# Even states of a selective scan take B from transposes of a repeated column; side work issued in fewer, later pieces

## The chip, the cores and the metric

The kernel runs on 1 core of one Trainium2 chip, in one launch. The metric is device time in microseconds from the first to the last instruction of that core; the time before is the median of 3 runs, 5304.8 us (5303.92 to 5304.85).

## The reference

Two layers, each added to its input after a group norm. Layer 0, in which the change lies, is a two-dimensional selective scan; layer 1 is a spectral attention block that is the same in both kernels. Layer 0, cut to what matters here:

```python
xin, z = split(x @ in_proj_w.T)                    # 4 images of 48 x 48 positions, d = 256
xc = silu(depthwise_conv3x3(xin) + conv_b)
xs = [xc, xc transposed, xc reversed, xc transposed and reversed]   # 4 directions, L = 2304
x_dbl = einsum('bkdl,kcd->bkcl', xs, x_proj_w)     # 40 rows: 8 for dt, 16 for B, 16 for C
dt = softplus(einsum('bkrl,kdr->bkdl', x_dbl[:8], dt_proj_w) + dt_proj_b)
for l in range(L):                                 # 16 states for each of the 256 channels
    h = h * exp(dt[l] * A) + (dt[l] * xs[l]) * B[l]
    y[l] = sum over the states of h * C[l]
y = the four directions, turned back and added, + Ds * xs
out = (layernorm(y) * silu(z)) @ out_proj_w.T
```

## The kernel before, in words

Channels lie on the 128 partitions in two halves (f = 0, 1), positions along the free axis. Each of 4 images has 4 directions in the order 0, 2, 1, 3 (ORDER), each direction 5 chunks of 480 positions (the last of them 384), each chunk 16 states: 80 chunks, 1280 states.

*The states.* The scan over positions is one DVE instruction per state over both halves (scan, L610), with a gap of two columns between them that carries the state from chunk to chunk. What goes into it:
- the decay, exp(dt * A), from ACT (decay, L598);
- the drive, dt * x * B. An **even** state makes it on DVE: spread (L549) copies one row of B to all partitions of the PSUM tile pb by a bf16 matmul of the chunk's tile bs with a column of pick, and drive_in (L568) multiplies du by pb into db. An **odd** state (turned) makes it on ACT and PE: scale (L575) multiplies dut, which is du transposed, by a column of bt, which is B transposed, and turn (L585) transposes the product into the PSUM tile da with 8 PE transposes.

After the scan, read_out (L619) multiplies h by C on POOL into hc (C is read back from memory, spread over the partitions, by fetch, L544), carry_on (L624) keeps the last column, and sum_up (L629) adds hc into the PSUM tiles yp with 8 PE transposes per state that accumulate. After state 15, put_away (L681) copies yp out on ACT, into the tile that held dut.

*The order.* The kernel writes out its own order: `on.` keeps every engine's instructions in the order of issue (so all of them have line L54 in the profile). advance (L735) takes one state per step and calls each stage for the state that entered so many steps before:

```python
    LAGS = (
        (3, fetch), (8, put_away), (4, drive_in), (5, scan), (4, decay_here), (3, spread), (4, turn), (3, decay_there),
        (2, extra), (2, scale), (5, read_out), (5, carry_on), (7, sum_up),
    )
```

*Side work.* What is not a state is written as generators that wait in the list later; piece (L708) runs one of them to its next yield. advance runs one piece at the end of every step, and extra (L719) one more in steps of odd states: three pieces for two states. A generator that yields FREE lets another one in; one that yields nothing goes on at the next piece. drain (L723) runs pieces until a generator is done. The generators:
- project_chunk (L400), for a chunk of the next direction: px (the 40 rows of x_dbl, and B twice more), the copies xd and bs, the products with less, dt from two pd matmuls, and bt from the transposes pt. bs holds B in bf16 with its first and second remainder, on rows 0, 64 and 96; the two products with less subtract from px what bs already holds, so that pick can add three bf16 parts to one nearly exact float32 row.
- turn_du (L375), which transposes du for the odd states, started by turning (L764);
- gather (L647), which turns yp's copy back and adds it to the direction before;
- back (L465), the layer norm and the output projection of a finished chunk, in direction 3;
- front (L265), input projection and convolution of the next image, and matrices (L288), which prepares layer 1 beside the last image; boot (L236) for the first.

All side matmuls go to one PSUM bank (tag pp, side, L152), which ACT or DVE must empty before the next one. The loop from L779 drives all this: in states 6 and 10 (or 9 and 12 of a direction's last chunk) it multiplies du for the next chunk on POOL (drive, L456), and after the second of these it calls turning, which first drains unfinished gathers.

Of the kernel before, what the change touches and what calls it, by code (L numbers as in the profile page):

```python
# [10 lines left out]
F32 = mybir.dt.float32  # L11
BF16 = mybir.dt.bfloat16
AF = mybir.ActivationFunctionType
ALU = mybir.AluOpType
# [8 lines left out]
D = 256  # L23
NF = D // 128
N = 16
R = 8
K = 4
NX = 112
BANK = 512
NH = 32  # L30

# [26 lines left out]
def first_layer(ctx, tc, io, x1_dram, sp_dram, d_w, d_m):  # L58
# [11 lines left out]
    small = ctx.enter_context(tc.tile_pool(name="l0_small", bufs=2))  # L70
    one = ctx.enter_context(tc.tile_pool(name="l0_one", bufs=1))
    two = ctx.enter_context(tc.tile_pool(name="l0_two", bufs=2))
    three = ctx.enter_context(tc.tile_pool(name="l0_three", bufs=3))
    four = ctx.enter_context(tc.tile_pool(name="l0_four", bufs=4))
    ring = ctx.enter_context(tc.tile_pool(name="l0_ring", bufs=RING))
    ps_a = ctx.enter_context(tc.tile_pool(name="l0_psa", bufs=1, space=PSUM))
# [26 lines left out]
    nc.scalar.dma_start(cb, io["conv_b"].rearrange("(f p) -> p f", p=128))  # L103

    w_xp = const.tile([128, K, NF, NX], F32, name="w_xp")
    on.gpsimd.memset(w_xp, 0.0)
    w_x = one.tile([128, K, NF, R + 2 * N], F32, tag="y", name="w_x")
    for k in range(K):
        nc.sync.dma_start(w_x[:, k], io["x_proj_wT"][k].rearrange("(f p) c -> p f c", p=128))
    for o, c0, c1 in ((0, R, R + 2 * N), (32, 0, R), (64, R, R + N), (96, R, R + N)):  # L110
        on.vector.tensor_copy(w_xp[:, :, :, o : o + c1 - c0], w_x[:, :, :, c0:c1])

    pick = const.tile([NX, N], BF16, name="pick")
    p3 = one.tile([NX, N], F32, tag="y", name="p3")
    on.vector.tensor_add(p3, ident[0:NX, 0:N], ident[0:NX, 64 : 64 + N])
    on.vector.tensor_add(pick, p3, ident[0:NX, 96 : 96 + N])

    less = const.tile([NX, 2, NX], BF16, name="less")
    on.gpsimd.memset(less, 0.0)
    on.vector.tensor_scalar(less[:, 0, 64:NX], ident[0:NX, 64:NX], -1.0, None, ALU.mult)  # L120
    on.vector.tensor_scalar(less[:, 1, 96:NX], ident[0:NX, 96:NX], -1.0, None, ALU.mult)
    b_dt = const.tile([128, K, NF], F32, name="b_dt")
    nc.scalar.dma_start(b_dt, io["dt_proj_b"].rearrange("k (f p) -> p k f", p=128))
    a_neg = const.tile([128, K * NF, N], F32, name="a_neg")
# [27 lines left out]
    def side(name):  # L152
        pool, tag = banks[0]
        if not begun[0]:
            banks.rotate(-1)
        return pool.tile([128, 512], F32, tag=tag, name=name)
# [218 lines left out]
    def turn_du(c):  # L375
# [3 lines left out]
        for h in range(0, 4, 2):  # L379
# [11 lines left out]
            for q, m, r in some:  # L391
                o = (q - h) * 256
                on.scalar.copy(c.dut[0:r, q : q + m], p[0:r, o : o + m * 256].rearrange("p (q d) -> p q d", d=256))

    def load_dt(b, k):
        w_dt = one.tile([32 + R, D], F32, tag="w_dt", name=f"w_dt{b}_{k}")
        nc.sync.dma_start(w_dt[32 : 32 + R], io["dt_proj_wT"][k])
        return w_dt

    def project_chunk(c, w_dt, xc):  # L400


        k, s, n = c.k, c.s, c.n
        src = at(xc, k, s, n)
        px = side(f"px{c.t}")
        for f in range(NF):
            on.tensor.matmul(
                like(px[0:NX, 0:n], k), w_xp[:, k, f], src[:, f], start=(f == 0), stop=(f == NF - 1)
            )
            yield  # L410
        xd = one.tile([32 + R, LC], F32, tag="xd", name=f"xd{c.t}")
        on.scalar.copy(xd[:, 0:n], px[0 : 32 + R, 0:n])
        c.cd = dram.tile([2 * N, LC], F32, tag="cd", name=f"cd{c.t}")
        nc.sync.dma_start(c.cd[:, 0:n], xd[0 : 2 * N, 0:n])

        c.bs = ring.tile([NX, LC], BF16, tag="bs", name=f"bs{c.t}")
        on.scalar.copy(c.bs[:, 0:n], px[0:NX, 0:n])
        for q in range(2):
            on.tensor.matmul(px[0:NX, 0:n], less[:, q], c.bs[:, 0:n], start=False, stop=True, skip_group_check=True)
            yield  # L420
            rows = slice(64 + 32 * q, NX)
            on.scalar.copy(c.bs[rows, 0:n], px[rows, 0:n])
        c.dt = ring.tile([128, NF, LC], F32, tag="dt", name=f"dt{c.t}")
        for f in range(NF):
            pd = side(f"pd{c.t}_{f}")
            on.tensor.matmul(
                pd[:, 0:n],
                w_dt[32 : 32 + R, f * 128 : (f + 1) * 128],
                xd[32 : 32 + R, 0:n],
                start=True,  # L430
                stop=True,
            )
            yield
            on.scalar.activation(c.dt[:, f, 0:n], pd[:, 0:n], AF.Identity, bias=b_dt[:, k, f : f + 1])

        c.bt = ring.tile([LB, 4, N], F32, tag="bt", name=f"bt{c.t}")
        pt = side(f"pt{c.t}")
        for q, r in blocks(n):
            on.tensor.transpose(pt[0:r, q * N : (q + 1) * N], xd[0:N, q * LB : q * LB + r], ident[0:N, 0:N])
        yield  # L440
        for q, m, r in runs(n):
            on.scalar.copy(c.bt[0:r, q : q + m], pt[0:r, q * N : (q + m) * N].rearrange("p (q n) -> p q n", n=N))

    def project(b, k, chunks, xc):

# [103 lines left out]
    def spread(u):  # L549

        c, i, n = u.c, u.i, u.c.n
        if i == N - 1:
            done[0] = c.number + 1
        if u.turned:
            return
        u.pb = ps_b.tile([128, 512], F32, tag="pb", name=f"pb{c.t}_{i}")
        on.tensor.matmul(
            u.pb[:, 0:n], pick[:, i : i + 1].to_broadcast([NX, 128]), c.bs[:, 0:n], start=True, stop=True
        )
        u.db = two.tile([128, NF * (LC + GAP)], F32, tag="db", name=f"db{c.t}_{i}")  # L560
        on.gpsimd.tensor_copy(u.db[:, n : n + GAP], before(u))

    def before(u):

# [53 lines left out]

    def read_out(u):  # L619
        c, i, n = u.c, u.i, u.c.n  # L620
        u.hc = three.tile([128, NF, LC], F32, tag="hc", name=f"hc{c.t}_{i}")
        on.gpsimd.tensor_mul(u.hc[:, :, 0:n], halves(u.h, n), u.cbc[:, :, 0:n].to_broadcast([128, NF, n]))

    def carry_on(u):  # L624
# [4 lines left out]
    def sum_up(u):  # L629

        c, i, n = u.c, u.i, u.c.n
        if i == 0:
            c.yp = [ps_y.tile([128, 512], F32, tag=f"yp{q}", name=f"yp{c.t}_{q}") for q in range(2)]
        for q, r in blocks(n):
            for f in range(NF):
                o = q % 2 * 256 + f * 128
                on.tensor.matmul(
                    c.yp[q // 2][0:r, o : o + 128],
                    u.hc[:, f, q * LB : q * LB + r],
                    ident,  # L640
                    start=(i == 0 and q % 2 == 0 and f == 0),
                    stop=(i == N - 1),
                    is_transpose=True,
                    skip_group_check=True,
                )

    def gather(c, yt):  # L647

# [68 lines left out]
                return  # L717

    def extra(u):  # L719
        if u.turned:  # L720
            piece()

    def drain(gen):  # L723
# [3 lines left out]

    decay_here, decay_there = partial(decay, turned=False), partial(decay, turned=True)
    LAGS = (
        (3, fetch), (8, put_away), (4, drive_in), (5, scan), (4, decay_here), (3, spread), (4, turn), (3, decay_there),  # L730
        (2, extra), (2, scale), (5, read_out), (5, carry_on), (7, sum_up),
    )
    window = deque([None] * 9, 9)

# [44 lines left out]
    for j, chunks in enumerate(directions):  # L779
        b, k = chunks[0].b, chunks[0].k  # L780
        if k == ORDER[0]:
            coming = None
        if k == ORDER[-1]:
            if b + 1 < B:
                drain(coming)
            images[b]["x"] = load_x(b, "xr")
        nxt = upcoming(j + 1) if j + 1 < len(directions) else None
        on.gpsimd.memset(carries[j % 2], 0.0)
        for m, c in enumerate(chunks):
            c.carry = carries[j % 2]  # L790
            for i in range(N):
                if k == ORDER[0] and b + 1 < B and m > 1 and coming is None and not any(g in later for g in backs):
                    coming = front(b + 1, images[b + 1])
                    later.append(coming)
                if k == ORDER[0] and b + 1 == B and m > 1 and coming is None and not any(g in later for g in backs):
                    coming = matrices()
                    later.append(coming)
                ahead = None
                if m + 1 < len(chunks):
                    f = (6, 10).index(i) if i in (6, 10) else None  # L800
                    if f is not None:
                        while not (j or chunks[m + 1].ready):
                            piece()
                        ahead = chunks[m + 1]
                elif nxt is not None:
                    f = (9, 12).index(i) if i in (9, 12) else None
                    if f is not None:
                        drain(nxt)
                        ahead = directions[j + 1][0]
                if ahead is not None:  # L810
                    drive(ahead, f)
                    if f:
                        turning(ahead)
                advance(Step(c, i))
                if not chunks[-1].ready and not j:
                    piece()
# [1288 lines left out]
```

## Time and profile before

| | |
|---|---|
| median of 3 runs | 5304.8 us |
| the profiled execution | 5305.0 us, span 5302.9 us |
| scans, first to last | from 80 to 4481 us |
| layer 1 after that | to 5303 us |
| mean granted TensorE clock | 0.870 |
| POOL waits for an hc that yp still reads | 261.3 us |
| PE waits for the copies of bs ahead of px<-bs,less | 151.1 us |
| DVE waits for pb ahead of db | 329.6 us |

The profile is of one execution. Engines: PE is the matmul side of TensorE and PEld its weight loads, which overlap; DVE is VectorE, ACT ScalarE, POOL GpSimd. A group of instructions is written out<-in by tile names. In brackets or after the bar stands the time that an engine was idle just before an instruction, with the instruction that ended it. The shares of the whole span are means over stretches with different limits, so a stretch is read by its own numbers. One float32 matmul call that is no transpose shows as two records; a transpose shows as one.

### The profile page before, as it was taken

Reading aid. Unit: us, or ns where it says so; the run is one execution under the profiler, and the core shown is the slowest. Engines: PE = TensorE matmul, PEld = TensorE weight load, DVE = VectorE, ACT = ScalarE, POOL = GpSimd, SP = SyncE. Lnnn points to the kernel's source line nnn. Section 1 sums busy time; section 2 is a strip of 40 time slices with the busy share of each in tenths; the row PEclk is TensorE's granted clock in tenths of the full one; section 3 lists DMA queues with packets and bytes.
Section 4 is the critical chain, followed back from the end, with each engine's and each line's share of the span. In section 5 each row is a group of like instructions: output and inputs, shape, how many; then the busy total and the mean of one; then the engine's idle time right before and its main releaser. Section 6 shows DMA issues by size and latency. Waiting matters only on the chain. (4 is left out here: it accounts for less than half of the span.)

```text
span 5302.9 us, 70751 instructions
## 1 busy us (share of the span) xinstructions
PE 4352.1 (82%) x24396; PEld 3035.5 (57%) x24396; DVE 3838.3 (72%) x2580; ACT 3771.0 (71%) x7327; POOL 3362.2 (63%) x3534
## 2 busy tenths in 40 slices
PE   6779888788798987888889888787888777688976
PEld 2556666555566666555666656565666655254543
DVE  1457778877787878768788777777888786456636
ACT  3667788878787878887888788877888876323344
POOL 2356767766777777766777677676777675146631
PEclk8879889888888888889899888988889898799977
DMA  1112222222222222222223222233333223216546
GB/s 33 53 51 68 83 70 81 76 70 67 76 76 84 76 75 74 75 66 85 70 78 87 74 72 74 67 88 74 84 85 86 71 78 88 54 28 160 127 117 152
DMA packets 306194, 417.78 MB, mean 79 GB/s; under 512 B 110804, under 2 KB 285012, under 8 KB 305260
## 3 DMA queue, kind: packets, MB, share of 16 engines
q1 hardware_dynamic: 300256, 410.19, 28.9%
q8 instruction: 193, 3.16, 0.2%
q10 hardware_dynamic: 5580, 3.08, 0.2%
q14 instruction: 165, 1.35, 0.1%
HBM read 377.99 MB, written 35.38 MB: 78 GB/s over the span
## 5 line engine op out<-in xcount | busy, mean ns | idle before, releaser
L54 POOL TENSOR_TENSOR hc<-h,cbc 128x960 f32<-128x960 f32 (+1 forms) x1280 | 2543.6, 1987 | 1280.0 <-DVE h L54 619.1
L54 DVE TENSOR_TENSOR_SCAN h<-da,carry,db 128x962 f32<-128x962 f32 (+1 forms) x640 | 1360.8, 2126 | 495.7 <-ACT da L54 465.4
L54 PEld LDWEIGHTS yp<-ident,hc 128*128 128x128 f32 (+1 forms) x9728 | 1259.9, 155 | 510.6 <-issue 366.2
L54 PE MATMUL yp<-ident,hc 128*128 128x128 f32 (+1 forms) x9728 | 1430.6, 299 | 22.2 <-POOL hc L54 17.0
L54 DVE TENSOR_TENSOR_SCAN h<-decay,carry,da 128x962 f32<-128x962 f32 (+1 forms) x640 | 1364.2, 2132 | 61.2 <-PE da L54 33.0
L54 ACT ACTIVATE scaled<-turned,bt 128x256 f32<-128x256 f32 (+1 forms) x2432 | 1036.1, 497 | 1.7
L54 DVE TENSOR_TENSOR db<-du,pb 128x960 f32<-128x960 f32 (+1 forms) x640 | 705.2, 1102 | 392.0 <-PE pb L54 329.6
L54 ACT ACTIVATE da<-dt,a_neg 128x480 f32<-128x480 f32 (+1 forms) x1280 | 827.2, 646 | 158.9 <-DVE h L54 137.3
L54 PE MATMUL da<-ident,scaled 128*128 128x128 f32 (+1 forms) x4864 | 711.8, 293 | 210.2 <-DVE h L54 174.2
L54 PEld LDWEIGHTS da<-ident,scaled 128*128 128x128 f32 (+1 forms) x4864 | 624.9, 156 | 434.8 <-ACT scaled L54 133.1
L54 ACT ACTIVATE decay<-dt,a_neg 128x480 f32<-128x480 f32 (+1 forms) x1280 | 790.9, 665 | 0.4
L54 PE MATMUL pc<-pad,cdiag 128*128 128x480 f32 (+1 forms) x630 | 290.6, 572 | 10.9 <-ACT pad L54 6.8
L54 POOL TENSOR_TENSOR du<-dt,xc 128x480 f32<-128x480 f32 (+1 forms) x160 | 206.3, 1290 | 108.1 <-ACT dt L54 108.1
L54 PE MATMUL pd<-xd,w_dt 8*128 8x480 f32 (+1 forms) x320 | 238.6, 837 | 35.5 <-ACT dt L54 18.2
L54 PE MATMUL pb<-bs,pick 112*128 112x480 bf16 (+1 forms) x640 | 251.4, 393 | 10.9 <-DVE db L54 10.7
L54 PE MATMUL px<-xc,w_xp 128*112 128x480 f32 (+1 forms) x320 | 223.8, 789 | 18.4 <-ACT xc L54 12.2
L1522 PE MATMUL acc<-v,attn_c 128*64 128x384 f32 x1152 | 210.3, 501 | 27.9 <-POOL v L1518 14.0
L54 ACT ACT_TABLE_LOAD x147 | 188.6, 1283 | 58.6 <-PE gv_l L54 34.9
L1518 POOL TENSOR_TENSOR v<-grep,xrep 128x768 f32<-128x768 f32 x96 | 174.7, 1823 | 87.4 <-PE acc L1522 46.9
L54 PEld LDWEIGHTS da<-carry,ident 128*128 128x128 f32 x1280 | 221.7, 217 | 0.0
L1514 DVE TENSOR_TENSOR v<-gp,xrep 128x1536 f32<-128x1536 f32 x96 | 168.1, 1756 | 73.9 <-PE acc L1522 41.2
L54 PE MATMUL da<-carry,ident 128*128 128x2 f32 x1280 | 211.5, 235 | 0.0
(382 smaller groups left out, 4544.8 us busy)
## 6 DMA issues: line engine op xcount, KB each, us to landing
cbc<-cd SPq DMA_DIRECT2D x1024, 240.0 KB
cbc<-cd SPq DMA_DIRECT2D x256, 192.0 KB
xrep<-dxt SPq DMA_DIRECT2D x48, 576.0 KB
grep<-dgt SPq DMA_DIRECT2D x16, 576.0 KB
x<-in_xT SPq DMA_DIRECT2D x16, 288.0 KB
xr<-in_xT SPq DMA_DIRECT2D x16, 288.0 KB
da_m<-a_m SPq DMA_DIRECT2D x24, 192.0 KB
a_m<-da_m SPq DMA_DIRECT2D x32, 144.0 KB
```

What stands on the lines that cost most here:

```text
L54: return lambda *args, **kw: self._tc.keep_in_program_order(emit(*args, **kw))
L1514: nc.vector.tensor_mul(v, gp[:, None, :, 0:NC].to_broadcast([128, 2, 2, NC]), x[:, :, 0:2])
L1518: nc.gpsimd.tensor_mul(v3, r[:, 2:3].to_broadcast([128, 2, NC]), x[:, :, 2])
L1522: nc.tensor.matmul(acc[c][64 * b : 64 * b + 64, 0:NC], attn_c[:, 2 * pair + b, g, q], v[:, b, c] if c < 2 else v3[:, b], start=first, stop ...
```

## The change

- **B for even states.** bs, less and pick go. spread makes pb with one PE transpose per block of 128 positions, whose input is one column of bt repeated 128 times. NX falls from 112 to 40.
- **bt.** The four transposes pt and their own yield go; in each of the two pd pieces two blocks of xd are transposed by an ordinary matmul with ident into spare columns of the same bank. w_dt becomes a constant tile with zeros in rows 0 to 31, and pd contracts over all 40 rows of xd instead of the 8 rows from 32. project_chunk has 4 yields instead of 7.
- **Side pieces on demand.** extra runs only where more than one generator waits.
- **turning** is called in state 13 instead of after the second drive.
- **The order in a step.** The sum of an even state has lag 8, so both sums of a pair stand in one step; put_away comes last; the copy of the carry into db is a stage of its own (open_db, lag 2) ahead of read_out instead of behind spread. hc has four buffers instead of three.

```diff
--- before.py
+++ after.py
@@ -25,7 +25,7 @@
 N = 16
 R = 8
 K = 4
-NX = 112
+NX = 40
 BANK = 512
 NH = 32
 
@@ -70,7 +70,6 @@
     small = ctx.enter_context(tc.tile_pool(name="l0_small", bufs=2))
     one = ctx.enter_context(tc.tile_pool(name="l0_one", bufs=1))
     two = ctx.enter_context(tc.tile_pool(name="l0_two", bufs=2))
-    three = ctx.enter_context(tc.tile_pool(name="l0_three", bufs=3))
     four = ctx.enter_context(tc.tile_pool(name="l0_four", bufs=4))
     ring = ctx.enter_context(tc.tile_pool(name="l0_ring", bufs=RING))
     ps_a = ctx.enter_context(tc.tile_pool(name="l0_psa", bufs=1, space=PSUM))
@@ -103,22 +102,12 @@
     nc.scalar.dma_start(cb, io["conv_b"].rearrange("(f p) -> p f", p=128))
 
     w_xp = const.tile([128, K, NF, NX], F32, name="w_xp")
-    on.gpsimd.memset(w_xp, 0.0)
     w_x = one.tile([128, K, NF, R + 2 * N], F32, tag="y", name="w_x")
     for k in range(K):
         nc.sync.dma_start(w_x[:, k], io["x_proj_wT"][k].rearrange("(f p) c -> p f c", p=128))
-    for o, c0, c1 in ((0, R, R + 2 * N), (32, 0, R), (64, R, R + N), (96, R, R + N)):
+    for o, c0, c1 in ((0, R, R + 2 * N), (32, 0, R)):
         on.vector.tensor_copy(w_xp[:, :, :, o : o + c1 - c0], w_x[:, :, :, c0:c1])
 
-    pick = const.tile([NX, N], BF16, name="pick")
-    p3 = one.tile([NX, N], F32, tag="y", name="p3")
-    on.vector.tensor_add(p3, ident[0:NX, 0:N], ident[0:NX, 64 : 64 + N])
-    on.vector.tensor_add(pick, p3, ident[0:NX, 96 : 96 + N])
-
-    less = const.tile([NX, 2, NX], BF16, name="less")
-    on.gpsimd.memset(less, 0.0)
-    on.vector.tensor_scalar(less[:, 0, 64:NX], ident[0:NX, 64:NX], -1.0, None, ALU.mult)
-    on.vector.tensor_scalar(less[:, 1, 96:NX], ident[0:NX, 96:NX], -1.0, None, ALU.mult)
     b_dt = const.tile([128, K, NF], F32, name="b_dt")
     nc.scalar.dma_start(b_dt, io["dt_proj_b"].rearrange("k (f p) -> p k f", p=128))
     a_neg = const.tile([128, K * NF, N], F32, name="a_neg")
@@ -392,8 +381,10 @@
                 o = (q - h) * 256
                 on.scalar.copy(c.dut[0:r, q : q + m], p[0:r, o : o + m * 256].rearrange("p (q d) -> p q d", d=256))
 
+    w_dt = const.tile([32 + R, D], F32, name="w_dt")
+    on.gpsimd.memset(w_dt, 0.0)
+
     def load_dt(b, k):
-        w_dt = one.tile([32 + R, D], F32, tag="w_dt", name=f"w_dt{b}_{k}")
         nc.sync.dma_start(w_dt[32 : 32 + R], io["dt_proj_wT"][k])
         return w_dt
 
@@ -413,33 +404,30 @@
         c.cd = dram.tile([2 * N, LC], F32, tag="cd", name=f"cd{c.t}")
         nc.sync.dma_start(c.cd[:, 0:n], xd[0 : 2 * N, 0:n])
 
-        c.bs = ring.tile([NX, LC], BF16, tag="bs", name=f"bs{c.t}")
-        on.scalar.copy(c.bs[:, 0:n], px[0:NX, 0:n])
-        for q in range(2):
-            on.tensor.matmul(px[0:NX, 0:n], less[:, q], c.bs[:, 0:n], start=False, stop=True, skip_group_check=True)
-            yield
-            rows = slice(64 + 32 * q, NX)
-            on.scalar.copy(c.bs[rows, 0:n], px[rows, 0:n])
+        c.bt = ring.tile([LB, 4, N], F32, tag="bt", name=f"bt{c.t}")
         c.dt = ring.tile([128, NF, LC], F32, tag="dt", name=f"dt{c.t}")
         for f in range(NF):
             pd = side(f"pd{c.t}_{f}")
             on.tensor.matmul(
                 pd[:, 0:n],
-                w_dt[32 : 32 + R, f * 128 : (f + 1) * 128],
-                xd[32 : 32 + R, 0:n],
+                w_dt[:, f * 128 : (f + 1) * 128],
+                xd[:, 0:n],
                 start=True,
                 stop=True,
             )
+            mine = blocks(n)[2 * f : 2 * f + 2]
+            for q, r in mine:
+                o = LC + q % 2 * N
+                on.tensor.matmul(
+                    pd[0:r, o : o + N], xd[:, q * LB : q * LB + r], ident[0 : 32 + R, 0:N], start=True, stop=True
+                )
             yield
             on.scalar.activation(c.dt[:, f, 0:n], pd[:, 0:n], AF.Identity, bias=b_dt[:, k, f : f + 1])
-
-        c.bt = ring.tile([LB, 4, N], F32, tag="bt", name=f"bt{c.t}")
-        pt = side(f"pt{c.t}")
-        for q, r in blocks(n):
-            on.tensor.transpose(pt[0:r, q * N : (q + 1) * N], xd[0:N, q * LB : q * LB + r], ident[0:N, 0:N])
-        yield
-        for q, m, r in runs(n):
-            on.scalar.copy(c.bt[0:r, q : q + m], pt[0:r, q * N : (q + m) * N].rearrange("p (q n) -> p q n", n=N))
+            for q, m, r in runs(sum(r for q, r in mine)):
+                o = LC + q * N
+                on.scalar.copy(
+                    c.bt[0:r, 2 * f + q : 2 * f + q + m], pd[0:r, o : o + m * N].rearrange("p (q n) -> p q n", n=N)
+                )
 
     def project(b, k, chunks, xc):
 
@@ -554,11 +542,17 @@
         if u.turned:
             return
         u.pb = ps_b.tile([128, 512], F32, tag="pb", name=f"pb{c.t}_{i}")
-        on.tensor.matmul(
-            u.pb[:, 0:n], pick[:, i : i + 1].to_broadcast([NX, 128]), c.bs[:, 0:n], start=True, stop=True
-        )
-        u.db = two.tile([128, NF * (LC + GAP)], F32, tag="db", name=f"db{c.t}_{i}")
-        on.gpsimd.tensor_copy(u.db[:, n : n + GAP], before(u))
+        for q, r in blocks(n):
+            on.tensor.transpose(
+                u.pb[:, q * LB : q * LB + r], c.bt[0:r, q, i : i + 1].to_broadcast([r, 128]), ident[0:r, 0:r]
+            )
+
+    def open_db(u):
+
+        c, i, n = u.c, u.i, u.c.n
+        if not u.turned:
+            u.db = two.tile([128, NF * (LC + GAP)], F32, tag="db", name=f"db{c.t}_{i}")
+            on.gpsimd.tensor_copy(u.db[:, n : n + GAP], before(u))
 
     def before(u):
 
@@ -618,7 +612,7 @@
 
     def read_out(u):
         c, i, n = u.c, u.i, u.c.n
-        u.hc = three.tile([128, NF, LC], F32, tag="hc", name=f"hc{c.t}_{i}")
+        u.hc = four.tile([128, NF, LC], F32, tag="hc", name=f"hc{c.t}_{i}")
         on.gpsimd.tensor_mul(u.hc[:, :, 0:n], halves(u.h, n), u.cbc[:, :, 0:n].to_broadcast([128, NF, n]))
 
     def carry_on(u):
@@ -643,6 +637,16 @@
                     is_transpose=True,
                     skip_group_check=True,
                 )
+
+    def sum_turned(u):
+
+        if u.turned:
+            sum_up(u)
+
+    def sum_plain(u):
+
+        if not u.turned:
+            sum_up(u)
 
     def gather(c, yt):
 
@@ -717,7 +721,7 @@
                 return
 
     def extra(u):
-        if u.turned:
+        if u.turned and len(later) > 1:
             piece()
 
     def drain(gen):
@@ -727,8 +731,8 @@
 
     decay_here, decay_there = partial(decay, turned=False), partial(decay, turned=True)
     LAGS = (
-        (3, fetch), (8, put_away), (4, drive_in), (5, scan), (4, decay_here), (3, spread), (4, turn), (3, decay_there),
-        (2, extra), (2, scale), (5, read_out), (5, carry_on), (7, sum_up),
+        (3, fetch), (2, open_db), (4, drive_in), (5, scan), (4, decay_here), (3, spread), (4, turn), (3, decay_there),
+        (2, extra), (2, scale), (5, read_out), (5, carry_on), (8, sum_plain), (7, sum_turned), (8, put_away),
     )
     window = deque([None] * 9, 9)
 
@@ -809,8 +813,9 @@
                         ahead = directions[j + 1][0]
                 if ahead is not None:
                     drive(ahead, f)
-                    if f:
-                        turning(ahead)
+                    driven = ahead
+                if i == 13 and (m + 1 < len(chunks) or nxt is not None):
+                    turning(driven)
                 advance(Step(c, i))
                 if not chunks[-1].ready and not j:
                     piece()
```

## The prediction

> **What bounds the kernel now.** I read the page first, then the stretch table (busy time of each engine in stretches I cut at the start of a scan), then the timeline inside the slow stretches, then the groups of instructions, and last the granted clock around single matmuls.
>
> ```profile
> span 5302.9 us, 70751 instructions
> PE 4352.1 (82%) x24396; PEld 3035.5 (57%) x24396; DVE 3838.3 (72%) x2580; ACT 3771.0 (71%) x7327; POOL 3362.2 (63%) x3534
> ```
>
> No engine is full over the whole span, so the limit changes from stretch to stretch. The scans run from 80 to 4481 us: 80 chunks of 16 states, that is 640 pairs of an even and an odd state. Here are six consecutive pairs of a chunk of direction 1 and one pair of a chunk of direction 3 (columns: stretch, its length, then busy us of PE, PEld, DVE, ACT, POOL with instruction counts, granted clock, DMA share, GB/s):
>
> ```profile
> 1967.60:1972.90 5.30, 3.39 (x27) 2.79 (x27) 5.30 (x4) 5.27 (x12) 4.48 (x5) 1.00 0.28 93
> 1983.50:1989.90 6.40, 6.14 (x32) 3.62 (x31) 5.37 (x4) 3.41 (x8) 5.24 (x6) 1.00 0.36 96
> 1989.90:1996.40 6.50, 4.73 (x26) 2.95 (x26) 5.52 (x4) 5.94 (x12) 5.49 (x7) 1.00 0.36 93
> 1996.40:2002.20 5.80, 4.95 (x37) 3.75 (x36) 5.53 (x4) 5.77 (x15) 3.89 (x5) 1.00 0.24 71
> 2002.20:2010.30 8.10, 7.46 (x49) 5.16 (x48) 5.46 (x3) 5.73 (x11) 5.77 (x7) 1.00 0.26 83
> 2010.30:2015.60 5.30, 3.38 (x29) 2.92 (x28) 5.28 (x3) 5.27 (x12) 4.43 (x5) 1.00 0.14 48
> 2259.30:2273.40 14.10, 13.45 (x64) 8.59 (x65) 5.56 (x3) 6.01 (x14) 8.17 (x9) 0.79 0.24 60
> ```
>
> A pair with no side work takes 5.30 us with DVE busy 5.30: two scans and the db product fill it, and PE has 1.9 us to spare. That is the floor. A pair with side pieces takes longer and DVE then waits. 640 pairs x 5.3 would be 3,390 us (a little less, as one chunk in five has 384 columns); the scans take 4,401. So about 1,000 us is what the side pieces cost, and the change works there. How they cost it:
>
> ```profile
> 1988.62 0.36 PE L54 MATMUL px<-bs,less 112*112 112x480 bf16 x1 [0.22 <-ACT bs L54]
> ...
> 1991.67 0.36 PE L54 MATMUL px<-bs,less 112*112 112x480 bf16 x1 [1.81 <-ACT bs L54]
> ```
> ```profile
> 2268.63 0.56 ACT L54 COPY yb<-pg 128x480 f32<-128x480 f32 x1 [3.30 <-PE pg L54]
> ...
> 2273.45 2.22 DVE L54 TENSOR_TENSOR_SCAN h<-da,carry,db 128x962 f32<-128x962 f32 x1 [5.49 <-ACT da L54]
> ```
>
> A side matmul goes to the one bank pp, ACT must empty it, and the next needs it back. Both queues run in order: PE stood 1.81 us for the copy of bs with pb and da behind it; ACT stood 3.30 us for pg with the exponential behind it, and the scan came 5.49 us late.
>
> **The change, part by part.** The profiled execution took 5305.0 us (span 5302.9), the median of the three runs is 5304.8; I sum against 5305.
>
> ```profile
> L54 PE MATMUL da<-ident,scaled 128*128 128x128 f32 (+1 forms) x4864 | 711.8, 293 | 210.2 <-DVE h L54 174.2 <-ACT scaled L54 31.7 <-ACT pad L54 1.5
> ...
> L54 PE MATMUL pb<-bs,pick 112*128 112x480 bf16 (+1 forms) x640 | 251.4, 393 | 10.9 <-DVE db L54 10.7
> ...
> L54 ACT CAST bs<-px 112x480 bf16<-112x480 f32 (+5 forms) x240 | 128.7, 536 | 45.4 <-PE px L54 43.3
> ...
> L54 PE MATMUL px<-bs,less 112*112 112x480 bf16 (+1 forms) x160 | 61.5, 384 | 152.2 <-ACT bs L54 151.1
> ...
> L54 PE MATMUL pt<-ident,xd 16*128 16x16 f32 (+1 forms) x304 | 41.7, 250 | 22.6 <-ACT dt L54 22.5
> ```
>
> 1. *pb by transposes.* 640 bf16 matmuls (251.4 us) become 2432 float32 transposes of at most 128 columns (8 even states x 3.8 blocks x 80 chunks). The row nearest is da: 711.8 / 4864 = 0.146 us each, so 356 us: +105 us of PE. In the quiet pair this lies in PE's 1.9 us of slack, unless pb comes late to the db product (DVE waited for pb 329.6 us in the whole run). In the pairs with side work PE is busy 73 to 96% of the time and it counts. Bounds: 0 and +105; I take 60%, **+65**.
>
> 2. *The split and its pieces go.* Per chunk 3 casts (128.7 us of ACT in all), 2 less matmuls (61.5 us of PE, and 151.1 us in which PE stood before them) and the separate pt piece go: project_chunk falls from 7 yields to 4. The transposition of B moves into the pd pieces as ordinary matmuls; a float32 one shows as two records in the trace (px has 320 for 160 calls), so 304 records become 608, +42 us of PE at pt's price, and the copies of bt rise from 2 to 3 per chunk of 480. What a piece costs: the chunk from 2187.3 to 2247.1 us took 59.8, which is 17.5 over 8 x 5.29, with 23 pieces in the issue loop: 0.76 each. The quiet chunk from 1942.0 to 1989.9 took 47.9, 5.6 over, with 13 pieces: 0.43 each. About 62 chunks carry back, front, matrices or boot: 62 x 3 x 0.76 = 141, from which I take the pd pieces growing by 42 x 60% = 25: **-116**. For the 15 quiet chunks, next point. Bounds: the regime of 0.43 everywhere less all 42 (-55), and -160 with the 151 us of waits gone.
>
> 3. *Fewer pieces at a time, turning later.* An odd state no longer runs its extra piece when only one generator is waiting: pairs with three pieces fall from 485 to 337 by the issue order. turning moves from the second drive (state 10, or 12) to state 13, so the gathers are done by themselves before it drains them: pieces issued in a burst by a drain fall from 72 to 10. The 14.1 us pair above is such a burst (pd, B's transposes, both gathers, du's transposes): 8.8 over the floor for about 5 pieces, where 0.76 x 5 would be 3.8, so 5 too many; 62 / 5 = 12 bursts: **-60**, bounds 0 and -60. In quiet chunks the 8.10 us pair also holds a gather and du's transposes; spacing them and dropping half of the excess of the three pairs before it gives 2.5 us for each of 15 chunks: **-38**, bounds -10 and -60. What is behind turning: the first scale of the next chunk (its state 1, two steps late) drains c.turn; three pairs lie between, enough for its three pieces. The two drive products stay where they are on POOL, and no DMA moves on SP.
>
> 4. *Sums of two states together; put_away last; open_db earlier; hc in four buffers.* The sums of the even state wait one step more, so in three-piece pairs two side pieces stand side by side on PE ahead of 16 sums, where 8 sums (1.05 us) stood between. The buffer added to hc covers that wait for POOL (before, POOL waited 261.3 us for yp to free an hc). put_away's copies come after scale, so ACT no longer waits for the last sum (26.9 us), and the copy into db comes one read_out earlier (DVE waited 54.6 us for it). Bounds -80 and +165 (see rivals); I take **0**, since the waits saved and the cover lost are of one size.
>
> 5. *pd with 40 rows instead of 8.* Same columns, same time. But see the clock around it:
>
> ```profile
> 2087.80:2091.20 3.40, 1.94 (x4) 0.58 (x4) 0.66 (x1) 1.00 0.26 83
> 2091.20:2094.60 3.40, 0.23 (x1) 0.00 (x0) 0.64 (x1) 0.50 0.26 66
> ```
>
> These are pd's records alone. Over the 1169 clock steps of 3.41 us between 480 and 4470 us in the trace, 14% of the steps after one without pd are at 0.50, and 88% of those after one with over 40% pd. The 8-row matmul seems to count as idle. About 105 half-speed steps hang on it, 39% of them all; pairs are 3.45 us longer per unit of clock lost (a fit over all pairs), 199 us in total, so 78 are at stake. What 40 rows do, no row shows. Bounds 0 and -78; I take a quarter, **-20**, as 40 is nearer 8 than 128.
>
> Sum: +65 - 116 - 60 - 38 + 0 - 20 = -169: 5305 - 169 = 5136. Layer 1 (from 4481 us) is untouched.
>
> **Rivals.**
> *A, the pieces are merely moved* (12%). What goes leaves time that the remaining pieces fill, because PE is the bound in the loaded chunks: only records count. PE then gets 105 + 42 - 62 = +85, and ACT's saving does not show; of the gains the bursts' 60 stays and the clock's 20. 5305 + 85 x 0.6 - 80 = 5276. For it: PE 95% busy where the next image's convolution runs. Against: PE at 82 to 84% in direction 3, where the excess is largest.
> *B, slower: two side pieces abreast* (11%). The second must wait until ACT, after four scaled (1.69 us), has emptied pp, and nothing lies between. If 1.05 us of cover is lost in half of the 337 three-piece pairs that is +177; with pb's +105 fully on the path and only the cheap bounds of parts 2 and 3 (-55, -10, -60, no clock): 5305 + 177 + 105 - 125 = 5462; halfway in both, 5321. It decides once a three-piece pair loses over 0.6 us. For: PE stood 1.81 us for bs in just this way. Against: convolution pieces need no copy between them, and the earlier second piece is ready earlier for ACT.
> *C, slower: the clock falls* (4%). Without the bf16 matmul and the less products the quiet stretches hold transposes only. At half clock a quiet pair's 3.39 us of PE becomes about 6.8, plus 0.3 for the longer pb: 7.1 against 5.3, 1.8 x some 200 pairs = +360 against -169: about 5496. Against it: from 2015.60 to 2026.20 us PE ran 6.78 us, all but 0.74 of it transposes, at clock 1.00; steps at half clock follow pd or idle time.
> [...]
>
> **How the numbers follow.** Forecast 73%, A 12%, B 11%, C 4%. Forecast's own range: the better bounds together seldom hold, so I go about 110 us either way: 5020 to 5250. The range takes in A and the mild half of B: 5020 to 5310. A change within 0.2% (11 us) can't be told from none. Faster: forecast and most of A, 83%; same 4%; slower 13%.
>
> **What would show it.** Right: quiet pairs still 5.3 us; a chunk of direction 1 at 44 to 46 us instead of 47.9; chunks of direction 3 at 56 to 58; PE's waits for bs gone and not replaced by waits for xd; no pair of 14 us; pb near 356 us; POOL's wait for yp not above 261. Wrong: PE's idle time before side matmuls grows (B), a mean clock well under 0.87 (C), or loaded chunks at their old length with PE fuller (A). A clock well above 0.87 would mean that part 5 was undersized.

## The result, and the profile after

The changed kernel takes 5071.1 us (median of 4 runs, 5056.6 to 5075.0) against 5304.4: a ratio of 0.9568, interval 0.953 to 0.9607, faster by 4.3%. The forecast was 5136 with a range from 5020 to 5310. The profiled execution took 5056.6 us, the fastest of the four and 248 below the profiled one of before; the mean granted clock rose from 0.870 to 0.918. All medians here are of fast executions; one of the four with pd over 8 rows took 17268.8 us and is left out.

The head of the page of the changed kernel, and its row of the clock in 40 slices:

```profile
span 5054.8 us, 73887 instructions
...
PE 4215.2 (83%) x26332; PEld 3091.3 (61%) x26332; DVE 3822.8 (76%) x2574; ACT 3635.6 (72%) x7167; POOL 3367.5 (67%) x3533
...
PEclk8999999989999999899999998999999997889977
```

PE has 1,936 more matmul records than before and yet 137 us less busy time, as much of its work ran at a higher clock: of the 4864 records of da, 861 ran at half clock before and 304 do now, and of the 320 of pd 179 and 12. ACT has 135 us less work; the casts were 128.7. The stretch table shows a pair with a piece of a gather in it, the next pair, which is the longest of its chunk of direction 1, that whole chunk, and direction 3 of the second image (five chunks):

```profile
1861.00:1866.30 5.30, 5.25 (x36) 3.74 (x34) 5.30 (x5) 5.27 (x15) 4.96 (x7) 1.00 0.44 92
1866.30:1873.40 7.10, 6.87 (x52) 5.42 (x49) 5.49 (x4) 4.63 (x9) 5.66 (x7) 1.00 0.35 105
1855.70:1899.70 44.00, 39.30 (x274) 29.83 (x275) 42.35 (x26) 37.52 (x77) 38.12 (x42) 1.00 0.32 89
1942.30:2226.60 284.30, 237.79 (x1405) 181.62 (x1405) 216.49 (x134) 228.38 (x431) 193.20 (x199) 0.90 0.28 73
```

The same two stretches of the kernel before:

```profile
1989.90:2037.60 47.70, 38.27 (x248) 28.57 (x248) 42.96 (x24) 39.02 (x79) 37.57 (x43) 0.96 0.28 80
2086.00:2372.70 286.70, 234.27 (x1271) 165.59 (x1271) 215.58 (x131) 234.93 (x439) 192.59 (x199) 0.89 0.27 71
```

In direction 1 the floor of 5.30 now holds even in the pair from 1861.0, which has a piece of a gather in it: PE is busy 5.25 of 5.30. The chunk is at 44.0 with DVE busy 42.35. Direction 3 is where it was: 284 against 287. Added up over all chunks by the starts of the scans, direction 1 of images 0 to 2 went from 763 to 677 us and direction 3 of all images from 1135 to 1101.

Groups of instructions (busy, mean ns, then idle time before), pd of the kernel before first and the rest after the change:

```profile
L54 PE MATMUL pd<-xd,w_dt 8*128 8x480 f32 (+1 forms) x320 | 238.6, 837 | 35.5 <-ACT dt L54 18.2 <-ACT bs L54 16.7
...
L54 PE MATMUL da<-ident,scaled 128*128 128x128 f32 (+1 forms) x4864 | 648.4, 277 | 107.5 <-DVE h L54 88.7 <-ACT scaled L54 14.9 <-ACT da L54 3.1
L54 PE MATMUL pb<-ident,bt 128*128 128x128 f32 (+1 forms) x2432 | 381.9, 279 | 5.6 <-DVE db L54 5.4
...
L54 PE MATMUL pd<-xd,w_dt 40*128 40x480 f32 (+1 forms) x320 | 171.5, 617 | 40.3 <-ACT xd L54 31.4 <-ACT bt L54 8.9
```

pb costs 381.9 - 251.4 = 131 us more of PE. da, whose instructions did not change, costs 63 less, and pd, of the same count and columns, 67 less: both ran less at half clock. The longest waits of PE after the change:

```profile
PE pdu L54 <- ACT turned L54: 122.0, 79, 5.8
PE pg L54 <- ACT turned L54: 93.2, 35, 9.1
PE da L54 <- DVE h L54: 88.7, 96, 1.6
```

The 151 us for bs are gone, and pd's wait for the copy xd that could have taken their place is 31.4. But two waits have grown: pdu's for the copy turned was 34.4, and pg's 0.2. POOL's wait for yp fell from 261.3 to 64.5. DVE's wait for pb rose from 329.6 to 397.8, so pb does come late in places. Pairs of 14 us or more did not vanish: 9 are left of 18.

### The profile page after: what moved, and what is told of

It is laid out like the page before. It is cut to its first block, busy times and chain, and to the rows that moved or that the text cites. A ratio compares the mean times of both kernels' runs of the same rounds, so it can differ in the third digit from the quotient of the medians.

```text
span 5054.8 us, 73887 instructions
## 1 busy us (share of the span) xinstructions
PE 4215.2 (83%) x26332; PEld 3091.3 (61%) x26332; DVE 3822.8 (76%) x2574; ACT 3635.6 (72%) x7167; POOL 3367.5 (67%) x3533
## 3 DMA queue, kind: packets, MB, share of 16 engines
q8 instruction: 208, 3.41, 0.3%
## 4 chain that ended last, share of the span: by engine, by line
PE 47%; ACT 23%; DVE 12%; issue 7%; POOL 3%; DMA 2%; SPq 1%; DVEq 0%; ACTq 0%; POOLq 0%
PE yp L54 12%; DVE h L54 7%; PE da L54 6%; ACT scaled L54 5%; PE pg L54 5%; PE pc L54 4%; ACT da L54 4%; ACT decay L54 4%; PE pd L54 3%; PE px L54 3%; DVE db L54 3%; PE pb L54 2%; ACT dt L54 2%; ACT L54 2%; ACT ws L54 1%
## 5 line engine op out<-in xcount | busy, mean ns | idle before, releaser
L54 PEld LDWEIGHTS yp<-ident,hc 128*128 128x128 f32 (+1 forms) x9728 | 1180.3, 148 | 301.2 <-issue 166.4
L54 PE MATMUL yp<-ident,hc 128*128 128x128 f32 (+1 forms) x9728 | 1297.5, 289 | 63.9 <-ACT turned L54 28.7
L54 DVE TENSOR_TENSOR db<-du,pb 128x960 f32<-128x960 f32 (+1 forms) x640 | 704.8, 1101 | 408.5 <-PE pb L54 397.8
L54 PE MATMUL da<-ident,scaled 128*128 128x128 f32 (+1 forms) x4864 | 648.4, 277 | 107.5 <-DVE h L54 88.7
L54 PEld LDWEIGHTS da<-ident,scaled 128*128 128x128 f32 (+1 forms) x4864 | 553.4, 146 | 136.5 <-ACT decay L54 52.0
L54 PEld LDWEIGHTS pb<-ident,bt 128*128 128x128 f32 (+1 forms) x2432 | 295.1, 143 | 218.2 <-issue 173.4
L54 PE MATMUL pb<-ident,bt 128*128 128x128 f32 (+1 forms) x2432 | 381.9, 279 | 5.6 <-DVE db L54 5.4
L54 PE MATMUL px<-xc,w_xp 128*40 128x480 f32 (+1 forms) x320 | 214.0, 768 | 16.3 <-ACT xc L54 12.3
L54 PE MATMUL pdu<-ident,du 128*128 128x128 f32 (+1 forms) x608 | 110.9, 308 | 127.1 <-ACT turned L54 122.0
L54 PE MATMUL pg<-ident,turned 128*128 128x128 f32 x608 | 110.8, 303 | 124.4 <-ACT turned L54 93.2
```

The lines of the kernel that those rows point to most:

```text
L54: return lambda *args, **kw: self._tc.keep_in_program_order(emit(*args, **kw))
```

## The experiments

Each run is given with its ratio to the kernel before on the same chip and the interval; the changed kernel is at 0.9568 (0.953 to 0.9607). Differences are those of the medians; by the ratios they come out within 15 us of these.

**pd over 8 rows again, in the changed kernel.**

```diff
-                w_dt[:, f * 128 : (f + 1) * 128],
-                xd[:, 0:n],
+                w_dt[32 : 32 + R, f * 128 : (f + 1) * 128],
+                xd[32 : 32 + R, 0:n],
```

> The changed kernel (5071) with pd over 8 rows again, all else kept. Theory 1 (the prediction's small price for the rows): +20, about 5090, mean clock 0.91. Theory 2 (the 8-row matmul counts as idle, and this halves the clock after it): the share of half-speed steps behind a step with over 40% pd goes from 21% back to some 80%, mean clock 0.88 to 0.89, +78 or more, about 5150.

5141.7 us, ratio 0.969 (0.9669 to 0.971), clock 0.899: +71 (65 by the ratios), near the 78 of the second theory. The share of half-speed steps behind pd did not go to 80%, though (47 of 107). The count in the prediction mixed cause and effect: pd is longer at half speed (the two records of a call over 480 columns took 1.07 us at 1.00 and 1.96 at 0.50 in the kernel before), so a step at half speed gets a larger share of pd, and half speed often lasts. Of the 65 half-speed steps that it counted in the kernel before, 60 came behind steps that were at half speed already. Counted from steps at full speed alone, 28 of 88 steps with over 40% pd are followed by half speed here, 9 of 59 in the changed kernel. (The 16-column matmuls that transpose B stand under the name pd too; they are the same in both.)

**40 rows in the kernel before**, with w_dt made as in the change and the same four lines.

> The kernel before (5304) with one edit: pd over 40 rows, 32 of the weights' rows zero. Theory 1: -20, about 5285. Theory 2: the half-speed steps behind pd go from 88% to about 20%, mean clock from 0.870 to about 0.90, -78, about 5226. If the rows only help together with the new order, the clock rises and the time stays within 10 us of 5304.

5277.0 us, ratio 0.9936 (0.9919 to 0.9953), clock 0.881: 30 us, near the first theory's 20. The half-speed steps behind pd did not go away there (54 of 66 behind steps with over 40% pd). But 53 of these 54 came behind steps at half speed; from full speed it was 1 of 13, against 5 of 14 in the kernel before. So the half speed begins elsewhere and lasts through pd. PE's waits for bs just ahead of pd are a likely place; no run shows it. The one edit is worth 30 us there and 71 in the changed kernel.

What half speed came behind can be seen in three clock steps of a quiet stretch of the kernel before (length, busy PE first, clock in the third column from the end):

```profile
2019.50:2023.00 3.50, 1.85 (x18) 1.88 (x18) 3.50 (x2) 2.52 (x6) 2.68 (x3) 1.00 0.40 115
2023.00:2026.40 3.40, 1.54 (x12) 0.92 (x9) 3.40 (x4) 3.22 (x6) 2.69 (x5) 1.00 0.23 75
2026.40:2029.80 3.40, 3.37 (x17) 3.39 (x18) 3.40 (x3) 2.25 (x6) 3.28 (x4) 0.50 0.34 87
```

PE busy 1.85 of 3.50 (53%): the next step keeps full speed. Busy 1.54 of 3.40 (45%): the next runs at half. Over the scans of the kernel before, with pd and pt not counted as busy: of 100 full-speed steps under 45% busy, 96 were followed by half speed; of 123 from 45 to 60%, 30; of 676 above 60%, none.

**One extra piece always.**

```diff
-        if u.turned and len(later) > 1:
+        if u.turned:
```

> The changed kernel with the extra piece in every step of an odd state, however many generators wait. Theory 1 (two pieces for two states fit behind the sums, a third makes PE and ACT wait for each other): chunks of direction 1 go from 42.6 to 45 us back to 46 or 47, +25 to +40 in all, about 5100. Theory 2 (the same pieces cost the same wherever they stand): within 10 us.

5171.6 us, ratio 0.9737 (0.9715 to 0.9759), clock 0.901: +100, two and a half times the most that either theory had. 65 of it lie in direction 1 of images 0 to 2 (741 us against 677). Two chunks of that direction:

```profile
1898.40:1946.60 48.20, 41.56 (x273) 32.55 (x272) 42.42 (x25) 37.41 (x77) 38.12 (x42) 0.93 0.31 81
1847.00:1898.40 51.40, 47.76 (x281) 38.29 (x282) 42.78 (x25) 38.16 (x79) 38.70 (x42) 0.81 0.28 78
```

The first is the chunk that took 44.0 us at clock 1.00 in the changed kernel. The same pieces stand in fewer pairs: some pairs are too full, and in others PE stands idle, the clock halves, and the next full pair runs at half speed. In direction 1 of images 0 to 2, 44 of 216 clock steps are at half speed here and 18 of 198 in the changed kernel. The clock fell behind 25 steps (8 in the changed kernel), and 20 of these begin in pairs that take no more than the floor's 5.3 us: in 10 of them PE's longest wait is for DVE, in 10 for a copy of ACT (turned ahead of pg, xd ahead of pd). The pair from 1847.0 to 1858.8 took 11.8 us at clock 0.50 with pd as its only side work.

**turning behind the second drive again.**

```diff
                     drive(ahead, f)
-                    driven = ahead
-                if i == 13 and (m + 1 < len(chunks) or nxt is not None):
-                    turning(driven)
+                    if f:
+                        turning(ahead)
```

> The changed kernel with turning behind the second drive (state 10 or 12) again. Theory 1 (bursts by drains are what it saved, 60 us): +40 to +60, about 5120, and pairs of some 14 us come back. Theory 2 (fewer project pieces already let the gathers end in time, so nothing is left to drain): within 10 us of 5071.

5056.5 us, ratio 0.9519 (0.9502 to 0.9535), which overlaps the changed kernel's: no loss, perhaps a small gain. The pieces issued in drains went from 10 to 62 by the issue order, and in sum that cost nothing; pairs of 14 us or more went from 9 to 11. By direction it is no null: 0 (images 1 to 3) and 2 are 28 and 30 us longer, 1 (images 0 to 2) and 3 are 23 and 29 shorter.

**The split put back, unused**: px over 112 columns, the casts, the less products and their two yields, with pb still made from bt. This kernel does work whose result nothing reads.

```diff
+        c.bs = one.tile([NX, LC], BF16, tag="bs", name=f"bs{c.t}")
+        on.scalar.copy(c.bs[:, 0:n], px[0:NX, 0:n])
+        for q in range(2):
+            on.tensor.matmul(px[0:NX, 0:n], less[:, q], c.bs[:, 0:n], start=False, stop=True, skip_group_check=True)
+            yield
+            rows = slice(64 + 32 * q, NX)
+            on.scalar.copy(c.bs[rows, 0:n], px[rows, 0:n])
         c.bt = ring.tile([LB, 4, N], F32, tag="bt", name=f"bt{c.t}")
```

> The changed kernel with the bf16 split put back beside it, its result unused: three casts, two less products and two yields per chunk, as before. Theory 1 (the pieces that went are worth about 116 us by the prediction, of which 2 of 3 come back here, and the waits before less): +80 to +120, about 5170, PE's wait for bs above 100 us. Theory 2 (the pieces only fill time that others take): under +40.

5200.2 us, ratio 0.9813 (0.9777 to 0.9849), clock 0.904: +129. The instructions of the tile bs, and what they waited for (us, times):

```profile
L54 PE MATMUL px<-bs,less x160: 322/363/627, 55.6 to 4164.8; 112*112 112x480 bf16 x128, 112*112 112x384 bf16 x32
its engine sat idle before it (us, times) until:
  ACT bs L54: 151.1, 131
```
```profile
L54 PE MATMUL px<-bs,less x160: 322/363/607, 56.4 to 4086.4; 112*112 112x480 bf16 x128, 112*112 112x384 bf16 x32
its engine sat idle before it (us, times) until:
  ACT bs L54: 158.4, 121
```

The first is the kernel before, the second this one: the wait of PE is back in full. No other wait of PE in the kernel before became so much shorter with the change. The run does not part the casts, the products and the yields from each other.

**pb's transposes twice.**

```diff
-        for q, r in blocks(n):
+        for q, r in blocks(n) * 2:
```

> The changed kernel with each of pb's transposes issued twice, so PE gets 2432 more records, some 380 us of busy time. If 60% of that lies on the path, as the prediction took: +230, about 5300. If PE has room (DVE is the floor in most pairs): under +100. If pb stands ahead of everything that DVE waits for: +380.

5180.7 us, ratio 0.9776 (0.974 to 0.9812), clock 0.923: +110.

```profile
L54 PE MATMUL pb<-ident,bt 128*128 128x128 f32 (+1 forms) x4864 | 650.0, 277 | 4.0 <-DVE db L54 3.9
```

650.0 - 381.9 = 268 us of PE, not 380: 110 ns for each of the 2432 more records, as the second set follows the first without a gap (PE is idle before pb for 4.0 us in all). 110 of 268 is 41% on the path. For the change's own +131 us that gives an estimate of +54; the replacement of pick's matmul itself was not undone.

**The order in a step.** Five runs take the last part of the change apart. The first puts one sum in each step and put_away second, as in the kernel before; the others take one edit each or add one.

```diff
-        (3, fetch), (2, open_db), (4, drive_in), (5, scan), (4, decay_here), (3, spread), (4, turn), (3, decay_there),
-        (2, extra), (2, scale), (5, read_out), (5, carry_on), (8, sum_plain), (7, sum_turned), (8, put_away),
+        (3, fetch), (8, put_away), (2, open_db), (4, drive_in), (5, scan), (4, decay_here), (3, spread), (4, turn),
+        (3, decay_there), (2, extra), (2, scale), (5, read_out), (5, carry_on), (7, sum_up),
```

> The changed kernel with one sum per step (lag 7) and put_away as second stage again, hc still in four buffers, open_db where the change put it. Theory 1 (the prediction's zero for this part): within 15 us of 5071. Theory 2 (both sums together give ACT the time to empty pp while PE works): +40 to +80, about 5130. Theory 3 (two side pieces abreast cost cover, rival B): 30 to 100 faster.

> The changed kernel with put_away ahead of extra and scale, sums still together. In the changed kernel PE waits 122 us for turned before pdu and 93 us before pg, which it did not before. Theory 1 (put_away's copies stand behind four scaled on ACT, and the gather's first pg waits for them): the 93 us fall under 40, and the time falls by 20 to 50, about 5035. Theory 2 (those waits lie where DVE is ahead anyway): within 10 us.

> The changed kernel with one sum per step (lag 7) and put_away left in the last place: one of the two edits of the run at 4991. If the two add (put_away alone gave 28 of the 80): about 5020. If put_away is all that sums apart need: near 5040 or above. If the sums alone are the whole of it: near 4991.

> The changed kernel with put_away as second stage of a step and both sums together in the last places: the other edit of the run at 4991 alone. put_away ahead of extra, sums together, gave 5043; sums apart, put_away last, gave 5059. If the place ahead of the exponentials is the whole gain and sums together cost nothing: about 4991. If early copies and sums apart each need the other: near 5040. If the even state's later sum now makes ACT wait for the last sum: 5060 or more.

| sums | put_away | us | ratio, interval |
|---|---|---|---|
| together | last (the change) | 5071.1 | 0.9568, 0.953 to 0.9607 |
| together | ahead of extra | 5042.8 | 0.9513, 0.9472 to 0.9555 |
| together | second | 5039.8 | 0.9521, 0.9488 to 0.9555 |
| apart | last | 5058.7 | 0.9546, 0.952 to 0.9572 |
| apart | second | 4991.1 | 0.9418, 0.9383 to 0.9453 |

Either edit alone gives 12 to 31 us, with intervals that touch the changed kernel's; both give 80, clear of all of them. So this part of the change as a whole is a loss of 80 us. One part of it can be seen in the timeline of the changed kernel:

```profile
2045.49 1.69 ACT L54 ACTIVATE scaled<-turned,bt 128x256 f32<-128x256 f32 x4
...
2047.09 1.10 ACT L54 COPY turned<-yp 128x512 f32<-128x512 f32 x3
...
2047.70 0.84 PE L54 MATMUL pg<-ident,turned 128*128 128x128 f32 x4 [2.12 <-ACT turned L54]
```

put_away's copies stand behind four scaled, the next piece is the gather that reads them, and PE stands 2.12 us for it. With put_away ahead of extra, pg's wait for turned falls from 93.2 to 54.9 us, not under 40 as expected. In the run at 4991 it is 16.4, and direction 3 of the second image takes 272 us instead of 284:

```profile
PE da L54 <- DVE h L54: 124.4, 138, 1.6
PE pdu L54 <- ACT turned L54: 68.3, 40, 6.5
PE pg L54 <- ACT y L54: 41.5, 36, 6.9
```
```profile
1917.80:2189.90 272.10, 233.64 (x1405) 171.58 (x1405) 215.11 (x133) 227.49 (x431) 192.88 (x199) 0.94 0.30 76
```

Why the two edits need each other is not shown. With put_away last and the sums apart, PE waits 117.3 us for turned before yp, as the first sum of the next chunk then stands in put_away's own step; that early sums need early copies fits this. What the sums together cost when the copies are early (49 us) fits rival B's side pieces abreast, but no run separates that from the later sum itself.

**turning early in the run at 4991**, and **pd over 128 rows in it**, 88 of them zeros in both operands:

> The faster kernel of the experiment with one sum per step and put_away early (4991), with turning behind the second drive again as well. If the delay of turning gives nothing, as its own undoing said (5056 against 5071): 4975 to 4995. If the delay matters once the sums are apart: 5010 or more.

> The kernel with one sum per step and put_away early (4991), with pd contracting over 128 rows, 88 of them zeros in both operands, instead of 40. If the clock's gate weighs a matmul by its rows, zeros included: the steps with pd count fully, mean clock from 0.927 to 0.935 or more, 10 to 25 faster. If 40 rows are already enough, or rows of zeros count for nothing: within 10 us and the same clock.

The first gives 5039.5 (0.9501, 0.9475 to 0.9527), a clear loss of 48: here the delayed turning is worth having, where in the changed kernel it was not. The second gives 4987.0 (0.9404, 0.9376 to 0.9432), the same time, with clock 0.931 for 0.927: of 65 full-speed steps with over 40% pd, one was followed by half speed, where the run at 4991 has 7 of 43. So the rest of what pd does to the clock is worth no time that can be told from none. The runs at 4991 and 4987 are the fastest.

## Why the prediction was right, and where its terms were not

The direction and the range held, and the sum of -169 became -233. The terms were less right than the sum: two gains (the rows, the fewer pieces) were taken far too small, and two parts that cost time were taken as free or as a gain (the order, the later turning). That these errors partly cancelled is luck. The numbers below are those of the runs that undo each part.

1. *pb by transposes, +65.* +131 us of PE instead of 105 (0.157 us for a record, not da's 0.146); 41% on the path instead of 60% (and 60% of 105 is 63, not 65). +54 by the doubled run: near.
2. *The split and its pieces, -116.* -129 by the run that puts two of the three yields back: near. The term left out that the clock is lower with the split in (0.904 against 0.918).
3. *Fewer pieces at a time, within -38.* -100. The prediction counted the excess of the quiet pairs, not what crowding does to the clock in the pairs next to them (44 of 216 clock steps at half speed for 18 of 198). *Turning later and its bursts, -60:* failed. Undoing it made the kernel 15 us faster, by intervals that overlap, although 52 more pieces were issued in drains. The 8.8 us that the 14 us pair took over the floor were read as the price of the burst, and they are not what spreading it saves.
4. *The order in a step, 0.* +80, the term furthest off. The prediction called put_away's later place a gain of 26.9 us for ACT and did not ask who reads the copies next: the gather does, in the same step. Moving put_away back alone gives 31 of the 80; why the rest needs the sums apart is open.
5. *40 rows, -20.* -71 in the changed kernel. The bound of -78 had been there; the quarter of it was a guess, and the count behind it was mostly an effect of the slow clock itself (60 of its 65 steps).

Rival A did not come: direction 1 reached the floor. B's place may be right, but its point of decision was not reached: 80 us over its 337 pairs would be 0.24 us each, an estimate, not 0.6. C did not come: the clock rose from 0.870 to 0.918, and the chunk from 1855.7 ran at 1.00. That the clock stays down through stretches of transposes, which its +360 assumed, no run shows: the quiet pair from 1884.0 to 1889.3 of the changed kernel ran at 1.00 with PE busy 3.76 us, all of it transposes but 0.31 for the carry. (The 6.78 us of PE named against it held two matmuls of the carry as well, 0.31 us each.) "Chunks of direction 3 at 56 to 58" was wrong: behind the first chunk of a direction they took 58 to 66 in images 0 to 2. In the run at 4991 most of them took 53 to 59, but the last still 62 to 64. "No pair of 14 us" was wrong as well.

The undone parts sum to -129 - 100 - 71 + 54 + 80 + 15 = -151 of the 233. The other 82 us (the piece of pt, the fourth hc, open_db, and what the parts do for each other) were not tried by themselves and stay open. That the parts do work on each other is plain: 40 rows gave 30 us in one kernel and 71 in the other, and the later turning lost 15 in one order and gained 48 in another.

## What to carry to other kernels

Work beside a loop was best spread thin here: pieces that fit into the room under the floor cost next to nothing (the pair from 1861.0 held a piece of a gather and took the floor's 5.30 us), while the same pieces crowded into some gaps cost twice, in the full gaps and in the clock that the idle ones lose (+100 us, at clock 0.901 for 0.918). A PE idle time should be priced with the half-speed step that can follow it, as it did behind 96 of 100 full-speed steps under 45% busy in the kernel before. And when a copy moves in a queue, the question is not only who stands behind it, but who reads it next and how soon.

## What the runs showed of the hardware

What follows is counted in the traces of these runs. The granted clock stands at 1.00 or 0.50 in every record of it (316 in the kernel before, 236 in the changed kernel), and each record but the last lasts a whole number of steps of 3.41 us. Behind a step at full speed it went with the share of that step in which PE was busy: in the scans of the kernel before, with pd and pt not counted as busy, half speed followed 96 of 100 steps under 45%, 30 of 123 from 45 to 60%, and none of 676 above. Behind a step at half speed the edge lay higher: of the changed kernel's half-speed steps without pd, all 57 that were under 80% busy were followed by half speed again, 6 of 13 from 80 to 90%, and none of the 80 over 90%. The transposes of yp start 109 ns apart at 1.00 and 213 at 0.50 (medians), so 80 to 90% busy at half speed is the work of 41 to 46% at full speed, by an estimate from these two numbers: in these steps about twice the busy time was needed to bring the clock back.

The float32 transposes of these kernels kept the full clock: of 731 full-speed steps without pd in the changed kernel that were over 60% busy, one was followed by half speed, and the quiet pairs among them hold nothing but transposes and the two columns of the carry. Busy time does not tell all of it, though. With put_away ahead of extra 14 of 772 such steps were followed by half speed, and all 14 hold 45% or more of the long float32 matmuls pg or pz; why half speed followed these is not shown.

Behind pd half speed came less often with more rows, zeros included: with 8 and 40 rows in the changed kernel, 28 of 88 and 9 of 59 full-speed steps with over 40% pd were followed by half speed; with 40 and 128 rows in the run at 4991, 7 of 43 and 1 of 65. The duration of pd did not go with the rows. The shortest record is the same with 8 rows (the first line) and with 40 (the second), 481 and 482 ns, and the medians differ (630 and 587) as more of the first ran at half clock:

```profile
L54 PE MATMUL pd<-xd,w_dt x320: 481/630/1165, 54.1 to 4025.8; 8*128 8x480 f32 x128, 8*128 8x384 f32 x32
L54 PE MATMUL pd<-xd,w_dt x320: 482/587/1166, 55.8 to 3949.6; 40*128 40x480 f32 x128, 40*128 40x384 f32 x32
```
